# The last pair of examples joins the Toom-Cook scheme, the last pairs take turns in two sets of PSUM banks, and setup work is cut into portions

## The chip, the core and the metric

The kernel runs on one core of a Trainium2 chip. The metric is the device time of one execution in microseconds (us). In the profile PE is TensorE (matmuls), PEld its weight loads, DVE is VectorE, ACT is ScalarE, POOL is GpSimd and SP is SyncE, whose queue issues the DMAs. PSUM is the memory that matmuls write[...].

## What is computed

For 128 examples with 64 channels and 1024 positions, `out = x + L3(L2(L1(L0(x))))`. Each layer is a one-dimensional convolution with three taps over 64 channels; its weight is scaled per example and input channel by a style vector `s`, and normalised per output channel:

```python
s = style @ mw.T + mb
weight = SCALE * w * s[:, None, :, None]
demod = lax.rsqrt(jnp.sum(weight * weight, axis=(2, 3)) + EPS)
weight = weight * demod[:, :, None, None]
# layer types: 'same', 'upsample', 'same', 'downsample', with fixed blurs
x = x + L0_cond_ref(...)          # all four layers, one after another
```

There is nothing nonlinear between the layers. For inner positions the four layers are therefore one convolution with nine taps and a constant, different for every example; a few positions at either end are computed layer by layer.

## The kernel before, in words

**Units of work.** Two examples make a pair (64 channels each, 128 partitions); there are 64 pairs, p = 0 to 63. Two pairs make a group of four examples, and the main loop goes through 32 groups, q = 0 to 31. A round of the loop makes the nine-tap weights of group q+2 and convolves pairs 2q to 2q+3 in part.

**Weights of a group.** `scale3`, `stage1`, `stage2` and `stage3` build them in three steps of matmuls (PSUM tiles psS, psR, psW), each brought to SBUF with a scale by ACT, or by ACT and VectorE in the first groups. The scales come from small tables of style and normalisation values (tA, tB, tC, t0, t02, t3). `residual` adds the identity that carries `+ x`, and `combine` forms three combinations of the taps (tile H, five VectorE instructions, lines 406 to 410).

**Convolution of a pair.** The nine taps fall into 3 x 3 parts, and the kernel multiplies the three-part polynomials in Toom-Cook's manner with five products instead of nine, each product a convolution with three taps. `pre1` and `pre2` form the input combinations from X: tile G on VectorE (lines 436 and 439), two slots of tile T on GpSimd (lines 443 and 444), the others on VectorE (lines 449 and 459). `convA12` and `convA3` run products 1 to 3 into psA; ACT copies them with scales (m1, m3; lines 505 to 507); `seed` combines them on VectorE (u and v at lines 515 and 516, then Y at line 526 and y1 at line 527). `seed` writes Y into PSUM, and `convB` adds products 0 and 4 on top of it by matmul. `output` (line 548) scales and shifts Y and y1 on ACT, and `store` sends the result off. Y is one tile of two banks, used by all pairs in turn: the seed of a pair waits until ACT has read the pair before it.

**The last pair.** Only pairs 0 to 62 take this way (`NT3 = NP - 1`). Pair 63 is convolved directly with its nine taps into a tile psD (`direct_taps`, line 572): four taps ahead of the last Toom-Cook pair's `convB`, five after it. `half_input` makes a halved copy of its input on ACT.

**Side work.** Style scales, normalisation and constants of the first 16 examples are made in the prologue, of the next 16 partly there, of the remaining 96 (REST) in the loop: `EXTRA[(q, 0)]` and `EXTRA[(q, 1)]` stand in the middle and at the end of round q, and `SLOTS[q]` gives small matmuls (psE) between the two products of a `convB`. The ends of the examples are computed in the same places in rounds 5 to 17 (`setup_x`, `setup0` to `setup3`, `ends0` to `ends3`, `rest0` to `rest3`).

**Order.** The order on every engine is the order in which the program issues instructions; no scheduler changes it. Each engine works through its own queue and waits at an instruction whose inputs or buffers are not ready. psA, and psR and psS of the prologue, share a pool of two buffers (`ps_conv`); the weight stages of the loop, psE and psD share one (`ps_w`).

Of the kernel before, what the change touches and what calls it, by code (L numbers as in the profile page):

```python
# [62 lines left out]
def kernel(  # L64
# [91 lines left out]
    Yv = Y[:, :, : 2 * NB].rearrange("c s (i j) -> c s i j", i=2)  # L156

    def zeros_to_y(sets, n):


        for i in range(sets):
            rows = HALF[i % 2]
            for cols in HALF:
                nc.tensor.matmul(  # L164
                    Y[cols, i % 2, :n], Z[rows, :C], Z[rows, :n], start=True, stop=True
                )
# [20 lines left out]
    def mod_scale(bs, src):  # L187
        m = mbs[:, :, None].to_broadcast([P, NL, bs.stop - bs.start])
        nc_v.scalar_tensor_tensor(
            sc[:, :, bs], by_layer(src, bs), SCALE, m, op0=ALU.mult, op1=ALU.add  # L190
        )
        nc_v.tensor_mul(ssq[:, :, bs], sc[:, :, bs], sc[:, :, bs])
# [28 lines left out]
    def var_newton(bs):  # L221

        newton(var[:, :, bs], dm[:, :, bs], nw[:, :, bs])
# [25 lines left out]
    def tables_s(bs):  # L249

        table(nc_g, tB, bs, ALT, DOWN, sc[:, 2, bs], sc[:, 1, bs])
        table(nc_g, t0, bs, ALT, ODD, sc[:, 0, bs], 1.0)
        table(nc_g, t02, bs, ALT, ODD, sc[:, 0, bs], -2.0)

    def tables_d(bs):
        first, last = slice(0, 2), slice(2, 4)
        table(nc_g, tC, bs, first, last, dm[:, 1, bs], dm[:, 0, bs])
        table(nc_g, t3, bs, ALT, ODD, dm[:, 3, bs], var[:, 3, bs])

    def tables(bs):  # L260
        table_A(bs, dm[:, 2, bs])
        tables_s(bs)
        tables_d(bs)
# [156 lines left out]
    NT3 = NP - 1  # L420

# [7 lines left out]
    def pre1(p):  # L429

        if p >= NT3:
            return
# [10 lines left out]
        nc_g.tensor_add(t[:, 2, :NJ], plane(g, 2), plane(g, 1))  # L443
        nc_g.tensor_sub(t[:, 3, :NJ], plane(g, 2), plane(g, 1))  # L444

    def pre2a(p, eng=nc_v):
        if p < NT3:
            X, t = Xs[p % NX], Ts[p]
            eng.tensor_sub(t[:, 4, :NJ], plane(X, 3), plane(X, 1))
            load(p + NX, slice(1, 3))  # L450

    def pre2b(p):
        if p >= NT3:
            return
# [10 lines left out]
    def product(p, m, ps):  # L465
# [3 lines left out]
        for g in range(3):  # L469
            for s, rows in enumerate(HALF):  # L470
                for h, cols in enumerate(HALF):
                    if m in (0, 4):
                        w = W[rows, r0, K * g + m // 2, :]
                    else:
# [3 lines left out]
                        ps[cols, s, :],  # L478
# [10 lines left out]
    def convA12(p):  # L489
        if p >= NT3:  # L490
            return
        ps = ps_conv.tile([P, 2, 512], F32, tag="u", name=f"psA{p}")
        m = [ps[:, :, i * NB : (i + 1) * NB] for i in range(3)]
        product(p, 1, m[0])
        product(p, 2, m[1])
        part[p] = m

    def convA3(p):
        if p >= NT3:
            return  # L500
        m = part[p]
        product(p, 3, m[2])
        m1 = m_tile("m1", p)
        m3 = m_tile("m3", p, (2, 2, NB))
        nc_a.activation(m1, m[0], AF.Copy, scale=-1.0)  # L505
# [4 lines left out]
    def seed1(p):  # L510
        if p >= NT3:
# [9 lines left out]
    def seed2(p):  # L521
        if p >= NT3:
# [3 lines left out]
        nc_v.tensor_add(Yv, u[:, :, None, :].to_broadcast([P, 2, 2, NB]), m3)  # L526
# [8 lines left out]
    def convB(p, between=None):  # L535
        product(p, 0, Yv[:, :, 0, :])
        if between:
            between()
        product(p, 4, Yv[:, :, 1, :])
# [3 lines left out]
    def output(p, s):  # L543

        b = 2 * p + s
        o = os[p][:, s, :]
        for dst, src in ((o[:, : 2 * NB], Y[:, s, : 2 * NB]), (o[:, 2 * NB :], y1s[p][:, s])):
            nc_a.activation(  # L548
                dst, src, AF.Identity, bias=oc[:, b : b + 1], scale=dm[:, 3, b : b + 1]
            )  # L550
# [3 lines left out]

    direct = {}

    def half_input(p):

        t = tpool.tile([P, 5, PL], F32, tag="T", name=f"X{p}_half")
        direct["half"] = t.rearrange("c m j -> c (m j)")[:, :NXC]  # L560
        nc_a.activation(direct["half"], Xs[p % NX], AF.Copy, scale=-0.5)

    def direct_taps(p, taps):
        if 0 in taps:
            direct["ps"] = unit(ps_w, "psD")
        W, X = Wq[p // 2][0], Xs[p % NX]
        for t in taps:
            src = direct["half"] if t % K == 2 else X
            for s, rows in enumerate(HALF):
                for h, cols in enumerate(HALF):  # L570
                    for n, i in enumerate((0, 2, 1)):
                        nc.tensor.matmul(  # L572
                            direct["ps"][s][cols, n * NB : (n + 1) * NB],
                            W[rows, p % 2, t, :],
                            plane(src, (i + t) % 3, NB * h + (i + t) // 3, NB)[rows],
                            start=(t == 0 and n == 0),
                            stop=(t == NT - 1),
                            skip_group_check=True,
                        )

    def direct_output(p):
        o = opool.tile([P, 2, HO], F32, tag="o", name=f"o{p}")
        for s in range(2):
            b = 2 * p + s
            src, d3, add = direct["ps"][s][:, :HO], dm[:, 3, b : b + 1], oc[:, b : b + 1]
            if s == 0:
                nc_a.activation(o[:, s], src, AF.Identity, bias=add, scale=d3)
            else:
                nc_v.tensor_scalar(o[:, s], src, d3, add, op0=ALU.mult, op1=ALU.add)
            nc.sync.dma_start(out[p, :, s], o[:, s])  # L590
# [29 lines left out]
    def vectors(bs, eng=nc_v):  # L620

        n = bs.stop - bs.start
        eng.tensor_mul(a1[:, bs], sc[:, 2, bs], sc[:, 1, bs])
        eng.tensor_mul(Da[:, bs], sc[:, 3, bs], dm[:, 2, bs])
        eng.tensor_mul(c0f[:, bs], dm[:, 1, bs], bb[:, 0:1].to_broadcast([P, n]))
        eng.tensor_mul(b1s[:, bs], sc[:, 2, bs], bb[:, 1:2].to_broadcast([P, n]))
        eng.tensor_mul(c2f[:, bs], sc[:, 3, bs], bb[:, 2:3].to_broadcast([P, n]))
# [67 lines left out]
    def blurred(g, src, k1, k3):  # L695

        for b, f in enumerate((k1, k3, k3, k1)):
# [3 lines left out]
    def setup_x():  # L701
        nc_v.tensor_tensor(Xm, Xe, spread(sc[:, 0, :], 8), op=ALU.mult)
# [7 lines left out]
    def setup1():  # L710
        blurred(g1, woi[:, 1], 0.25, 0.75)

    def setup2():
        blurred(g3, wio[:, 3], 0.125, 0.375)
# [105 lines left out]
    BOTH = nc_a, nc_v  # L820
    zeros_to_y(2, 512)
# [8 lines left out]
    tables_s(PART[0])  # L830
    var_matmul(PART[0], pm[0][1])
    blur(0, 1)
    var_root(PART[0], pm[0][1])

    zeros_to_y(6, 256)
# [4 lines left out]
    scale3(1)  # L840
    blur(1, 3)
    var_inverse(PART[0])
    var_newton(PART[0])
    tables_d(PART[0])
    vectors(PART[0], nc_g)
# [4 lines left out]
    pre1(0)  # L850
    stage2(0, None, BOTH)
    pre2a(0, nc_g)
    mod_matmul(PART[1], pm[1][0])
    mod_scale(PART[1], pm[1][0])
    zeros_to_y(2, 512)
    const_first(0, PART[0])
    pre1(1)
    pre2a(1, nc_g)
# [3 lines left out]
    var_root(PART[1], pm[1][1])  # L862
# [3 lines left out]
    var_inverse(PART[1])  # L866
# [5 lines left out]
    const_rest(2, PART[0], const_of(2, PART[0]))  # L872
    stage2(1, ps_conv)
    pre2b(0)
    convA12(0)
    convA3(0)
    pre1(2)
    pre2a(2, nc_g)
# [3 lines left out]
    pre2b(1)  # L882
# [3 lines left out]
    var_newton(PART[1])  # L886
    tables(PART[1])
    vectors(PART[1], nc_g)
    residual(1)
    combine(1)  # L890
    pre2b(2)
    pre1(3)
    nc.sync.dma_start(Xe, x_ends)
    zeros()
# [5 lines left out]
    def scales_and_constant(matmul, l):  # L900
        def f(ps):
            matmul(REST, ps[0])
            const_matmul(l, PART[1], ps[1])

        return f

    def const1(l):
        const_rest(l, PART[1], raw[turn[0]][:, 1, :])

    SLOTS = {  # L910
        0: (scales_and_constant(mod_matmul, 0), NL * n, n1),
        1: (scales_and_constant(var_matmul, 1), NL * n, n1),
        2: (lambda ps: const_matmul(2, PART[1], ps[0]), n1),
# [3 lines left out]
        8: (ends0, HB * 6, HB * 6),  # L917
        10: (ends1(0), HB * 5, HB * 5),
        11: (ends1(1), HB * 4, HB * 4),
        14: (ends2, HB * 8, HB * 8),  # L920
        16: (ends3, HB * 3, HB * 3),
    }
    def after(side):
        return raw[turn[0]][:, side, :]


    EXTRA = {
        (0, 1): lambda: (mod_scale(REST, after(0)), const1(0)),
        (1, 1): lambda: (var_root(REST, after(0)), const1(1)),
        (2, 0): lambda: var_inverse(REST, slice(0, 1)),  # L930
        (2, 1): lambda: (const_rest(2, PART[1], after(0)), var_inverse(REST, slice(1, 2))),
        (3, 0): lambda: var_inverse(REST, slice(2, 3)),
        (3, 1): lambda: var_inverse(REST, slice(3, 4)),
        (4, 0): lambda: (var_newton(REST), tables(REST), vectors(REST, nc_g)),
        (5, 0): setup_x,
        (5, 1): lambda: (const_rest(0, REST, after(0)), setup0()),
        (6, 0): setup1,
        (6, 1): lambda: const_rest(1, REST, after(0)),
        (7, 0): setup2,
        (7, 1): lambda: (const_rest(2, REST, after(0)), setup3()),  # L940
        (8, 1): lambda: rest0(0),
        (9, 0): lambda: rest0(1),
        (10, 1): lambda: rest1(0),
        (11, 1): lambda: rest1(1),
        (12, 1): lambda: rest1_bias(0),
        (13, 0): lambda: rest1_bias(1),
        (14, 1): lambda: rest2(0),
# [121 lines left out]
```

## Time and profile before

| | |
|---|---|
| median of three runs | 520.89 us (520.56 to 521.82) |
| the profiled execution's own time | 520.98 us |
| its span, first to last instruction | 519.2 us |
| busy: PE, DVE, ACT, POOL | 501.2, 459.7, 364.8, 158.4 us |
| granted TensorE clock, mean | 0.997 |
| moved by DMA | 70.92 MB, mean 137 GB/s |

"Busy" counts every moment in which at least one instruction of the engine is under way. A PE that is busy is not always at its best rate[...]. Every fp32 matmul of the program stands in the trace as two records: 12 matmuls of a product are 24 records. The listed durations of neighbouring VectorE instructions overlap slightly, so what an instruction costs its queue is the distance of two starts.

### The profile page before, as it was taken

What the parts mean: (1) busy time and instruction counts of PE and PEld (TensorE: products, weight loads), DVE (VectorE), ACT (ScalarE), POOL (GpSimd) and SP (SyncE); (2) the same over time, 40 slices, a digit from 0 to 9 for tenths busy, and PEclk for the clock granted to TensorE, in tenths of its full rate; (3) what the DMA queues carried; (4) which work ended last, traced back from release to release, by engine and by line L of the source; (5) the groups of instructions that cost most, each with busy time, mean ns of one, the idle gap of its engine ahead of it and who ended that gap; (6) DMA issues with size and microseconds to landing.
All of it is one profiled execution on the core that took longest, in us unless ns stands there. A gap on an engine that the chain in (4) does not pass through costs nothing.

```text
span 519.2 us, 28593 instructions
## 1 busy us (share of the span) xinstructions
PE 501.2 (97%) x12724; PEld 478.0 (92%) x12724; DVE 459.7 (89%) x839; ACT 364.8 (70%) x908; POOL 158.4 (31%) x201
## 2 busy tenths in 40 slices
PE   8998999997899999999999999999999999999996
PEld 4897999997899799999979999999999999999996
DVE  5999989999999999889989989999998898888750
ACT  3365787776675777777767767787777777777742
POOL 3678122384323323212331313332222221222100
PEclk9998999999999999999999999999999999999999
DMA  8215443453534544434544445554444444453122
GB/s 250 85 46 168 147 152 115 137 166 109 139 117 133 164 129 139 147 114 138 164 113 138 135 118 177 167 164 135 144 144 161 142 148 134 159 166 110 68 101 82
DMA packets 37163, 70.92 MB, mean 137 GB/s; under 512 B 4144, under 2 KB 28464, under 8 KB 37040
## 3 DMA queue, kind: packets, MB, share of 16 engines
q1 hardware_dynamic: 36960, 68.85, 43.2%
q8 instruction: 100, 1.64, 1.4%
q10 hardware_dynamic: 80, 0.25, 0.1%
q14 instruction: 23, 0.19, 0.1%
HBM read 35.46 MB, written 33.62 MB: 133 GB/s over the span
## 4 chain that ended last, share of the span: by engine, by line
PE 78%; DVE 15%; ACT 3%; issue 2%; DMA 1%; DVEq 0%; ACTq 0%
PE psA L477 25%; PE Y L477 19%; PE psR L331 13%; PE psW L368 11%; PE psS L300 5%; DVE Y L526 3%; PE psD L572 2%; PE psE L725 2%; DVE y L527 2%; DVE G L436 1%; DVE T L459 1%; ACT o L548 1%; DVE G L439 1%; PE Y L164 1%; DVE H L409 1%
## 5 line engine op out<-in xcount | busy, mean ns | idle before, releaser
L477 PE MATMUL psA<-T,H 64*64 64x170 f32 x4536 | 190.1, 304 | 0.0
L477 PEld LDWEIGHTS psA<-T,H 64*64 64x64 f32 x4536 | 173.5, 133 | 0.5 <-issue 0.3
L443 POOL TENSOR_TENSOR T<-G 128x342 f32<-128x342 f32 x63 | 59.1, 938 | 318.1 <-DVE G L439 243.7
L477 PE MATMUL Y<-T,Wf 64*64 64x170 f32 x3024 | 129.4, 306 | 10.2 <-DVE Y L526 10.2
L477 PEld LDWEIGHTS Y<-T,Wf 64*64 64x64 f32 x3024 | 114.3, 133 | 15.1 <-DVE Y L526 13.8
L548 ACT ACTIVATE o<-Y,oc,dm 128x340 f32<-128x340 f32 x126 | 80.1, 636 | 43.8 <-PE Y L477 41.5
L526 DVE TENSOR_TENSOR Y<-u,m 128x680 f32<-128x680 f32 x63 | 69.7, 1106 | 30.5 <-ACT o L548 30.5
L278 ACT ACTIVATE Wf<-psW,t 128x256 f32<-128x256 f32 (+1 forms) x252 | 75.3, 381 | 24.7 <-PE psW L368 24.4
L368 PE MATMUL psW<-R,par_oi 64*64 64x256 f32 (+3 forms) x1536 | 91.7, 350 | 0.4 <-ACT Wf L278 0.4
L331 PE MATMUL psR<-S,E 64*64 64x192 f32 (+1 forms) x2304 | 89.4, 299 | 0.3 <-ACT S L278 0.3
L331 PEld LDWEIGHTS psR<-S,E 64*64 64x64 f32 x2304 | 81.7, 133 | 1.3 <-ACT S L278 0.7
L368 PEld LDWEIGHTS psW<-R,par_oi 64*64 64x64 f32 x1536 | 73.6, 133 | 7.8 <-ACT Wf L278 1.1
L444 POOL TENSOR_TENSOR T<-G 128x342 f32<-128x342 f32 x63 | 73.4, 1165 | 0.0
L548 ACT ACTIVATE o<-y,oc,dm 128x170 f32<-128x170 f32 x126 | 66.4, 527 | 0.0
L278 ACT ACTIVATE R<-psR,tC 128x448 f32<-128x448 f32 x63 | 36.5, 630 | 40.7 <-PE psR L331 40.7
L436 DVE SCALAR_TENSOR_TENSOR G<-X 128x688 f32<-128x688 f32 x63 | 56.1, 891 | 0.1
L459 DVE TENSOR_TENSOR T<-G 128x684 f32<-128x684 f32 x63 | 55.1, 875 | 0.0
L527 DVE SCALAR_TENSOR_TENSOR y<-m,v 128x340 f32<-128x340 f32 x63 | 49.1, 779 | 0.0
L300 PE MATMUL psS<-wd,par_oi 64*64 64x192 f32 x768 | 40.3, 324 | 0.0
L505 ACT ACTIVATE m<-psA 128x340 f32<-128x340 f32 x63 | 28.9, 459 | 7.0 <-PE psA L477 4.1
L300 PEld LDWEIGHTS psS<-wd,par_oi 64*64 64x64 f32 x768 | 32.3, 134 | 1.5 <-ACT wd L278 0.6
L439 DVE SCALAR_TENSOR_TENSOR G<-X 128x342 f32<-128x342 f32 x63 | 33.4, 531 | 0.0
(131 smaller groups left out, 476.1 us busy)
## 6 DMA issues: line engine op xcount, KB each, us to landing
out<-o SPq DMA_DIRECT2D x128, 255.0 KB, 3.4
X<-in_x SPq DMA_DIRECT2D x60, 344.0 KB, 3.3
X<-in_x SPq DMA_DIRECT2D x60, 172.0 KB, 3.2
X<-in_x SPq DMA_DIRECT2D x4, 516.0 KB, 6.9
Xe<-in_x_ends SPq DMA_DIRECT2D x1, 512.0 KB, 4.7
par_oi<-in_params_oi SPq DMA_DIRECT2D x2, 208.0 KB, 5.3
par_io<-in_params_io ACTq DMA_DIRECT2D x1, 240.0 KB, 4.3
par_io<-in_params_io SPq DMA_DIRECT2D x1, 240.0 KB, 4.9
```

Source lines behind the costliest of these rows:

```text
L278: nc_a.activation(dst, src, AF.Copy, scale=f)
L300: nc.tensor.matmul(ps[r][cols, k * C : (k + K) * C], woi[rows, 2, k, :], src[rows, :], start=(k == 0), stop=(k == K - 1), skip_group_check ...
L331: nc.tensor.matmul(ps[r][cols, lo * C : (lo + m) * C], E[rows, e + 2, :], src[rows, a, :], start=(n == 0), stop=(n == 8), skip_group_check ...
L368: nc.tensor.matmul(ps[r][cols, (lo - t_lo) * C : (hi - t_lo) * C], woi[rows, 0, k, :], rt[c][rows, lo - k : hi - k, :], start=(k == order[0]),
L436: nc_v.scalar_tensor_tensor(g[:, PL:], X[:, : 2 * PL], 0.5, X[:, PL:], op0=ALU.mult, op1=ALU.subtract)
L443: nc_g.tensor_add(t[:, 2, :NJ], plane(g, 2), plane(g, 1))
L444: nc_g.tensor_sub(t[:, 3, :NJ], plane(g, 2), plane(g, 1))
L459: nc_v.tensor_sub(t[:, 0:2, :NJ], both(a, PL), both(b, 1))
L477: nc.tensor.matmul(ps[cols, s, :], w, Ts[p][rows, SLOT[m], j : j + NB], start=(g == 0 and m not in (0, 4)), stop=(g == 2), skip_group_chec ...
L526: nc_v.tensor_add(Yv, u[:, :, None, :].to_broadcast([P, 2, 2, NB]), m3)
L527: nc_v.scalar_tensor_tensor(y1, m3[:, :, 0, :], 2.0, v, op0=ALU.mult, op1=ALU.add)
L548: nc_a.activation(dst, src, AF.Identity, bias=oc[:, b : b + 1], scale=dm[:, 3, b : b + 1])
```

## The change

1. Pair 63 takes the Toom-Cook way too. `half_input`, `direct_taps` and `direct_output` go away; `pre1`, `pre2`, `convA`, `seed`, `convB` and `output` of pair 63 come in.
2. The last pairs get a second set of banks. When the weights of the last group are done, `ps_w` has no more use: two of its banks become Y2, for pairs 60 and 62, while pairs 61 and 63 keep Y. Four zero matmuls prepare Y2. The last two rounds are reordered: `convA12` of pair 63 comes ahead of `convB` of pair 61, the seeds of 62 and 63 come earlier, VectorE does the second output of pairs 61 and 62, and pair 63 is output in parts by ACT and VectorE together.
3. The style matmul for all examples after the first 16 is done once in the prologue (`LATER`) and copied to SBUF by ACT, instead of once there for 16 examples and once in slot 0 for 96.
4. The side work of the loop is cut into smaller portions and spread further: what GpSimd did in round 4 in one piece (tables and vectors of REST) goes in portions into rounds 1 to 5, VectorE's normalisation of REST into rounds 2 to 5 by layers, and the work on the ends, in the slots 8, 10, 11, 14 and 16 before, into the slots 9, 12, 14, 19 and 24, with its setup and rest steps in rounds 6 to 25.
5. In the prologue, `pre1` and `pre2a` of pairs 0 and 1 run on VectorE alone, `pre2a` of pair 2 as well; several steps change places, and the first half of round 0 does the second part of pair 1's seed ahead of the column work of pairs 3 and 4.

The core of the diff:

```diff
+    def y_bank(p, s):
+        return Y2[p][s] if p in Y2 else Y[:, s]
...
-    NT3 = NP - 1
...
-    def pre1(p):
-
-        if p >= NT3:
+    def pre1(p, eng=nc_g):
+
+        if p >= NP:
             return
...
-        nc_g.tensor_add(t[:, 2, :NJ], plane(g, 2), plane(g, 1))
-        nc_g.tensor_sub(t[:, 3, :NJ], plane(g, 2), plane(g, 1))
+        eng.tensor_add(t[:, 2, :NJ], plane(g, 2), plane(g, 1))
+        eng.tensor_sub(t[:, 3, :NJ], plane(g, 2), plane(g, 1))
...
+        if p in Y2:
+            for s in range(2):
+                nc_v.tensor_add(
+                    blocks(y_bank(p, s)[:, None, :]), uu[:, s : s + 1], m3[:, s : s + 1]
+                )
+        else:
+            nc_v.tensor_add(blocks(Y), uu, m3)
...
+    mod_matmul(LATER, pm[1][0])
 
-    zeros_to_y(6, 256)
+    zeros_to_y(4, 256)
...
+    nc_a.copy(raw[0][:, 0, :n_later], pm[1][0][:, :n_later])
...
+    mod_scale(PART[1], raw[0][:, 0], LATER)
+    for of in (table_B, vector_a1, table_0, table_02, vector_b1, vector_c2):
+        of(PART[1])
     stage2(0, None, BOTH)
-    pre2a(0, nc_g)
-    mod_matmul(PART[1], pm[1][0])
-    mod_scale(PART[1], pm[1][0])
+    pre1(0, nc_v)
+    pre2a(0)
...
     EXTRA = {
...
-        (4, 0): lambda: (var_newton(REST), tables(REST), vectors(REST, nc_g)),
-        (5, 0): setup_x,
-        (5, 1): lambda: (const_rest(0, REST, after(0)), setup0()),
-        (6, 0): setup1,
...
+        (1, 0): lambda: (table_B(REST), vector_a1(REST)),
+        (1, 1): lambda: (var_root(REST, after(0)), const_rest(0, PART[1], after(1))),
+        (2, 0): lambda: (var_inverse(*layers(2, 3)), table_0(REST), vector_b1(REST)),
+        (2, 1): lambda: (const_rest(1, PART[1], after(0)), var_newton(*layers(2, 3))),
+        (3, 0): lambda: (table_A(REST, dm[:, 2, REST]), table_02(REST), vector_c2(REST)),
+        (3, 1): lambda: (const_rest(2, PART[1], after(0)), var_inverse(*layers(1, 2))),
+        (4, 0): lambda: (var_inverse(*layers(0, 1)), vector_Da(REST)),
+        (4, 1): lambda: (var_newton(*layers(0, 2)), table_C(REST), vector_c0(REST)),
+        (5, 0): lambda: var_inverse(*layers(3, 4)),
+        (5, 1): lambda: (
+            const_rest(0, REST, after(0)),
+            var_newton(*layers(3, 4)),
+            table_3(REST),
+        ),
...
         if q == NQ - 1:
+            seed(p + 1)
+        output(p, 1, nc_a if q < NQ - 1 else nc_v)
+        if q == NQ - 1:
+            store(p, 0)
+            store(p, 1)
+
+            convB(p + 1)
+            for i in (2, 0, 1):
+                for r, eng in enumerate(BOTH):
+                    output(p + 1, r, eng, ((i, i + 1),))
             for i in range(2):
-                store(p, i)
-            direct_taps(p + 1, range(4, NT))
-            direct_output(p + 1)
+                store(p + 1, i)
             break
...
+            store(p, 0)
+            seed2(p + 1)
+            pre2(p + 3)
+            store(p, 1)
+            pre2b(p + 2)
+            pre1(p + 4)
...
+        if q == NQ - 2:
+            convA12(p + 3)
         side = SLOTS.get(q)
         convB(p + 1, (lambda: slot(*side)) if side else None)
+        if q == NQ - 2:
+            seed(p + 2)
...
+        if c == NQ - 1:
+
+            banks = unit(ps_w, "Y2")
+            Y2[p + 2] = Y2[p + 4] = banks
+            zeros_to_y(2, 2 * NB, p + 2)
```

## The prediction

> **What bounds the kernel now.** The page first: engines, the chain that ended last, TensorE's costliest groups.
>
> ```profile
> PE 501.2 (97%) x12724; PEld 478.0 (92%) x12724; DVE 459.7 (89%) x839; ACT 364.8 (70%) x908; POOL 158.4 (31%) x201
> PE 78%; DVE 15%; ACT 3%; issue 2%; DMA 1%; DVEq 0%; ACTq 0%
> L477 PE MATMUL Y<-T,Wf 64*64 64x170 f32 x3024 | 129.4, 306 | 10.2 <-DVE Y L526 10.2
> ```
>
> TensorE bounds most of the span, but it waits for one thing, VectorE's seed of Y. The windows view by rounds (starts of stage2 from the timeline) says where:
>
> ```profile
> 97.41:112.61 15.20, 14.63 (x393) 13.77 (x385) 14.91 (x26) 11.22 (x29) 8.01 (x11) 1.00 0.40 107
> 112.61:130.06 17.45, 14.70 (x396) 13.87 (x391) 17.31 (x29) 11.36 (x30) 9.54 (x14) 1.00 0.48 142
> 130.06:146.29 16.23, 14.79 (x396) 14.43 (x391) 15.93 (x34) 11.46 (x30) 4.52 (x5) 1.00 0.48 133
> 146.29:162.18 15.89, 14.79 (x397) 14.43 (x391) 15.62 (x30) 11.47 (x30) 4.83 (x5) 1.00 0.45 129
> 392.71:407.10 14.39, 14.39 (x393) 14.13 (x386) 12.66 (x25) 11.21 (x29) 3.60 (x4) 1.00 0.48 148
> ```
>
> (Length, then PE, PEld, DVE, ACT, POOL busy.) A late round takes 14.39 us, all TensorE; rounds 4 to 7 take 15.2 to 17.5 with VectorE full: there VectorE bounds. Its timeline gives the first seeds of rounds 5 to 8:
>
> ```profile
> 123.55 1.04 DVE L526 TENSOR_TENSOR Y<-u,m 128x680 f32<-128x680 f32 x1
> ...
> 139.78 1.04 DVE L526 TENSOR_TENSOR Y<-u,m 128x680 f32<-128x680 f32 x1
> ...
> 155.64 1.07 DVE L526 TENSOR_TENSOR Y<-u,m 128x680 f32<-128x680 f32 x1
> ...
> 172.16 1.06 DVE L526 TENSOR_TENSOR Y<-u,m 128x680 f32<-128x680 f32 x1
> ```
>
> Distances 16.23, 15.86 and 16.52; by starts, the side work between them is 2.26, 1.90 and 2.52. The rest is 13.97, 13.96 and 14.00: **a saturated VectorE round costs 13.97 us**, only 0.42 under TensorE's 14.39. Side work beyond 0.42 a round, plus TensorE's own side matmuls, lengthens the round.
>
> The end has a third limit:
>
> ```profile
> 499.99 5.59 PE psD L572 x92
> 507.75 6.93 PE psD L572 x116
> DVE o L589 <- PE psD L572: 11.8, 1, 11.8
> ```
>
> In the chain of waits the direct convolution's 216 records take about 12.6 us, 58 ns each; a Toom-Cook product takes 0.87 us for 24, 36 ns.[...]
>
> [...] y1 takes 0.50 us alone and 1.22 beside GpSimd's T, two instructions of H 1.15 instead of 0.56. So moving column work off GpSimd returns part of its price.
>
> **The tail.** Removed: 216 direct records (12.6 us) and the half copy (1.05 on ACT, hidden). Added for pair 63: five products, 120 records at 36 ns (4.3 us), and on VectorE line 436 0.79, 439 0.42, 449 0.42, 459 0.78, u and v 0.84, Y 0.86, y1 0.42, by starts. Followed queue by queue from `convB(59)`, which ends at 489.75:
> - Four zero matmuls into Y2: eight 64x512 records took 1.09 at 16 us, so 340 columns take 0.7. They need psW empty, which it is at 488.7. `convA(61)` ends at 493.0.
> - VectorE does `pre2(62)`, then the added `pre1(63)`, to 490.4; u, v and Y2 for pair 60, with GpSimd's T beside them, to 492.5, early enough; then `combine(31)` as before, to 496.4. `convB(60)` ends at 494.8, `convA(62)` at 497.4.
> - `convA12(63)` needs the psA buffer of pair 61, and VectorE reaches u and v of 61 only after `combine(31)` and `pre2(63)`, at 498.5: a new wait of 1.1, with `convB(61)` and `convA3(63)` queued behind it. The matmuls end at 500.3, `convB(61)` at 502.0, `convA3(63)` at 502.9; Y2 for 62 was ready at 501.5, so `convB(62)` ends at 504.6.
> - ACT's m3 of 63 comes behind `output(61, 0)`, at 504.0; Y of 63 at 504.9; `convB(63)` ends at 506.7. The last part of the output, 170 columns (0.53 on ACT), ends at 507.35.
>
> Before, the last output ended at 515.52. The stores behind it are the same size and keep their 3.7 us. **Tail: -8.1 us** (-9 to -5.5[...]).
>
> **The loop, rounds 2 to 25.** TensorE's side matmuls are the same work in other slots, and cost what they did; removed is slot 0's style matmul (1.3), but VectorE bounds that round, so I count it as nothing. What GpSimd gets in portions, about 1 to 2.6 us a round, lies in its idle time (7 us ahead of a T). Round 4 before also had 8 us of GpSimd tables, which pushed T onto H: its distance was 17.41 - 13.97 - 2.33 = 1.1 above the rule. VectorE's stall before, distances minus 14.39 and minus the slot of that round: 0.55, 0.82, 3.02, 1.69, 1.32, 1.98 (rounds 2 to 7) and 0.98 (13), 10.4 in all. After, side work per round, from rows of the same kind (reciprocal 0.67 of 96 columns, Newton 0.75 for one layer and 1.0 for two, constants 0.29 or 0.46, tA 0.45, half of `setup_x` 0.6, half of `setup1` 0.72, `setup0` 0.67, `setup3` 0.62, each `rest0` 1.1, `rest1` 0.96, each bias step 1.29, each `rest2` 1.37):
>
> | round | side | after 0.42 and the slot | stall |
> |---|---|---|---|
> | 1 | 0.56 | -0.71 | 0 |
> | 2 | 1.71 | 1.19 | 0.48 |
> | 3 | 1.41 | 0.89 | 0.89 |
> | 4 | 1.67 | 1.25 | 1.25 |
> | 5 | 1.88 | 1.31 | 1.31 |
> | 6, 7 | 1.06 each | 0.49 each | 0.98 |
> | 8 | 0.67 | 0.25 | 0.25 |
> | 9, 10 | 1.72, 1.82 | -0.64 (slot 1.94), 1.40 | 0.76 |
> | 11 | 0.72 | 0.30 | 0.30 |
> | 12 to 16 | 0.96, 0, 0.96, 1.29, 1.29 | slots 1.6, 1.4; lead up to 1.6 | 0.14 |
> | 17 | 1.44 | 1.02 | 1.02 |
> | 19 to 25 | two of 1.37, 0.7, 1.2 | slots 2.6, 2.7 cover | 0 |
>
> Sum 7.4. **Loop: -3.0 us**; up to -5.5 if shorter side work lets VectorE regain its lead[...].
>
> **Prologue and round 0.** VectorE gains seven T instructions of 342 columns (0.42 each by starts, 2.9 us)[...]. The style matmul for 112 columns in place of 16 has no row; by 16 records of 96 columns in 1.34 us it costs at most 1.4 more, less two sets of zeros dropped (0.9), and delays `stage1(0)` by 0 to 0.5. The ACT copy of 448 columns (as R, 0.63) falls ahead of S at 11.84 and costs nothing there. On VectorE, H(1) can start at 33.6, behind the last ACT part of its weights (33.2) and the residual; H takes 3.0[...], then line 449, u, v 1.26, line 459 0.78, G 1.22, normalisation of the second part 1.6: pair 1's seed at 42.7, before at 44.47. The gap of 2.6 us ahead of `convB(1)` shrinks to about 1.3. But `pre2(3)`, `pre2b(2)` and `pre1(4)`, 3.2 us, are only put behind that seed. From it to seed 3 the queue holds, by starts, columns 1.98 + 1.22 + 1.2 + 1.22, u, v, Y, y1 of pair 2 2.54, residual and H 3.4, scales 1.06, columns 2.42, u and v 0.84, with y1 of pair 1 0.42: 16.3[...]. Seed 3 starts at 60.0 to 61.5, before at 60.70: TensorE waits for it in rounds 0 and 1 instead of once, and `convB(3)` starts where it did. SP's loads of X for pairs 4 to 7 are issued some microseconds apart from before, long ahead of use; the load of Xe and GpSimd's memsets go into round 1, used from round 6 on. **Start: 0** (-1.5 to +2).
>
> **Sum.** -8.1 - 3.0 + 0 = -11.1 on a span of 519.2; the profiled execution took 520.98 (1.78 around the span), the median is 520.89. So **509.8 us**.
>
> **Rivals.**
> - *The debt only moves.* VectorE does the same side work, and in saturated rounds each microsecond reaches TensorE wherever it stands; for it speaks 0.42 of room a round, against it that rounds 17 to 31 have idle VectorE. Tail -8.1, start +1.5: 514.3.
> - *The banks turn, but the seeds are late*, i.e. the change doesn't do what it says at the end: VectorE's queue (pair 63's column work, the split Y, two outputs) holds seeds 61 to 63, each `convB` waits about 1 us more. Tail -5, loop -3: 513.
> - *VectorE becomes the bound in rounds 2 to 25 (slower).* [...] With +0.44 the table's stalls become about 13.3, still a gain. The point is a round of about 14.65, +0.7; at +1.0 some 20 rounds add 0.56 each, the stalls reach 24.5 and the sum is +6: 527. Only round 4 before, with 8 us of GpSimd work, was that slow.
>
> **How the numbers follow.** Forecast 0.63, first rival 0.2, second 0.12, third 0.05. Differences within 0.3% (1.6 us) can hardly be told from none here; little lies there. Faster 0.93, same 0.02, slower 0.05. The forecast's own ends (-9 - 5.5 - 1.5 to about -4) and the first two rivals give 505 to 515.5.
>
> **What would show it.** Right: no psD, last output some 3.7 us ahead of the end, 120 records in its place, a wait ahead of pair 63's psA; first seeds of rounds 2 to 5 some 15.3 to 15.7 us apart and of 6 to 8 about 14.9; DVE full until round 11 or so. Wrong: rounds above 15.7 through 10 (third rival), or `convB` of 61 to 63 waiting over 1 us each (second); a start that ends `convB(3)` beyond 64 or before 60.

## The result, and the profile after

The changed kernel takes 518.68 us in the median of six runs (515.94 to 519.51), the kernel before 521.41 (520.56 to 521.82): ratio 0.9943, interval 0.9918 to 0.9969. It is faster, but by about 2.9 us (518.19 against 521.07 when both were run again) where 11.1 were forecast. Its runs spread over 3.6 us, those of before over 1.3. The profiled execution is the fastest of the six: 515.94 us, span 514.1, mean granted clock 0.993.

The page of after, in the lines that answer to those of before (engines, chain that ended last, TensorE's matmuls into Y):

```profile
PE 492.9 (96%) x12612; PEld 467.9 (91%) x12612; DVE 476.7 (93%) x869; ACT 364.0 (71%) x908; POOL 159.7 (31%) x196
PE 65%; DVE 20%; ACT 3%; issue 2%; DVEq 0%
L481 PE MATMUL Y<-T,Wf 64*64 64x170 f32 x3072 | 131.3, 307 | 12.0 <-DVE Y L547 10.9
```

The 216 direct records are gone and the 120 of pair 63 are in, but VectorE's share of the chain rose from 15 to 20%, and TensorE waits for its seeds of Y as long as before (10.9 us against 10.2). The windows by rounds, 4 to 7 and a late one:

```profile
99.18:114.52 15.34, 14.86 (x392) 14.27 (x387) 15.17 (x28) 11.25 (x29) 5.32 (x6) 1.00 0.48 140
114.52:130.53 16.01, 14.70 (x397) 13.88 (x391) 15.80 (x28) 11.37 (x30) 7.08 (x8) 1.00 0.48 133
130.53:146.51 15.98, 14.78 (x396) 14.42 (x390) 15.74 (x30) 11.46 (x30) 6.15 (x7) 1.00 0.44 136
146.51:161.50 14.99, 14.79 (x397) 14.43 (x392) 14.82 (x27) 11.47 (x30) 4.84 (x5) 1.00 0.47 143
389.44:403.86 14.42, 14.42 (x392) 13.90 (x386) 13.88 (x24) 11.23 (x29) 4.50 (x5) 1.00 0.54 155
```

(Length, then PE, PEld, DVE, ACT, POOL busy, the granted clock, and DMA.) VectorE is still full through round 7. The first seeds of rounds 5 to 8 in VectorE's timeline:

```profile
124.04 1.02 DVE L547 TENSOR_TENSOR Y<-u,m 128x680 f32<-128x680 f32 x1
...
139.99 1.05 DVE L547 TENSOR_TENSOR Y<-u,m 128x680 f32<-128x680 f32 x1
...
154.99 1.03 DVE L547 TENSOR_TENSOR Y<-u,m 128x680 f32<-128x680 f32 x1
...
169.99 1.06 DVE L547 TENSOR_TENSOR Y<-u,m 128x680 f32<-128x680 f32 x1
```

They are 15.95, 15.00 and 15.00 us apart; less the forecast's side work (1.88, 1.06, 1.06) that is 14.07, 13.94 and 13.94. The rule of 13.97 us for a saturated VectorE round holds, as far as the side work was forecast rightly.

Cut by the starts of stage2 of groups 0, 10 and 31 (the last two open rounds 8 and 29), the profiles show where the gain is and where it went. The last column is VectorE's idle time within the stretch from stage2(0) to stage2(10), its length less its busy time there.

| kernel | stage2(0) at | to stage2(10) | to stage2(31) | to the end | VectorE idle |
|---|---|---|---|---|---|
| before | 12.42 | 149.76 | 316.89 | 40.1 | 5.72 |
| after | 11.79 | 149.71 | 317.26 | 35.3 | 6.40 |
| after, again | 13.49 | 150.61 | 317.34 | 35.4 | 7.80 |

The whole gain is in the end, 4.8 us. The loop's shorter rounds gained nothing: rounds 2 to 7 took 91.37 us in place of 93.89, but from stage2(0) to the start of round 2 after took 58.34 in place of 55.87.

### The profile page after: what moved, and what is told of

Same layout as the page of the kernel before. It is cut to its first block, busy times and chain, and to the rows that moved or that the text cites. A ratio compares the mean times of both kernels' runs of the same rounds, so it can differ in the third digit from the quotient of the medians.

```text
span 514.1 us, 28399 instructions
## 1 busy us (share of the span) xinstructions
PE 492.9 (96%) x12612; PEld 467.9 (91%) x12612; DVE 476.7 (93%) x869; ACT 364.0 (71%) x908; POOL 159.7 (31%) x196
## 4 chain that ended last, share of the span: by engine, by line
PE 65%; DVE 20%; ACT 3%; issue 2%; DVEq 0%
PE psA L481 21%; PE Y L481 18%; PE psR L337 11%; PE psW L374 9%; PE psS L306 4%; DVE Y L547 3%; DVE T L463 3%; DVE y L548 2%; DVE G L440 2%; PE psE L724 2%; ACT o L572 2%; DVE G L443 1%; DVE u L528 1%; DVE T L453 1%; DVE H L413 1%
## 5 line engine op out<-in xcount | busy, mean ns | idle before, releaser
L481 PE MATMUL psA<-T,H 64*64 64x170 f32 x4608 | 193.9, 304 | 1.0 <-DVE v L529 1.0
L481 PEld LDWEIGHTS psA<-T,H 64*64 64x64 f32 x4608 | 176.9, 133 | 2.2 <-issue 1.6
L447 POOL TENSOR_TENSOR T<-G 128x342 f32<-128x342 f32 x62 | 57.0, 920 | 312.8 <-DVE G L443 266.7
L481 PE MATMUL Y<-T,Wf 64*64 64x170 f32 x3072 | 131.3, 307 | 12.0 <-DVE Y L547 10.9
L481 PEld LDWEIGHTS Y<-T,Wf 64*64 64x64 f32 x3072 | 115.9, 133 | 18.0 <-DVE Y L547 15.0
L572 ACT ACTIVATE o<-Y,oc,dm 128x340 f32<-128x340 f32 (+1 forms) x126 | 79.8, 633 | 48.0 <-PE Y L481 47.2
L547 DVE TENSOR_TENSOR Y<-u,m 128x680 f32<-128x680 f32 x62 | 67.2, 1083 | 17.2 <-ACT o L572 17.0
L448 POOL TENSOR_TENSOR T<-G 128x342 f32<-128x342 f32 x62 | 82.0, 1323 | 0.0
L548 DVE SCALAR_TENSOR_TENSOR y<-m,v 128x340 f32<-128x340 f32 x64 | 60.2, 940 | 0.0
L463 DVE TENSOR_TENSOR T<-G 128x684 f32<-128x684 f32 x64 | 56.3, 881 | 0.0
L528 DVE SCALAR_TENSOR_TENSOR u<-psA,m 128x340 f32<-128x340 f32 x64 | 32.1, 502 | 0.8 <-ACT m L520 0.8
```

The costliest lines, as they stand in the source:

```text
L447: eng.tensor_add(t[:, 2, :NJ], plane(g, 2), plane(g, 1))
L448: eng.tensor_sub(t[:, 3, :NJ], plane(g, 2), plane(g, 1))
L463: nc_v.tensor_sub(t[:, 0:2, :NJ], both(a, PL), both(b, 1))
L481: nc.tensor.matmul(ps[s][cols], w, Ts[p][rows, SLOT[m], j : j + NB], start=(g == 0 and m not in (0, 4)), stop=(g == 2), skip_group_check=True,
L547: nc_v.tensor_add(blocks(Y), uu, m3)
L548: nc_v.scalar_tensor_tensor(y1, m3[:, :, 0, :], 2.0, v, op0=ALU.mult, op1=ALU.add)
```

## The experiments

Medians are compared with those of before taken beside them (520.88 to 521.17). In the expectations "stage2(2)" means the start of round 2, and "the last full round" and "round 31" start at stage2(31).

**The end alone.** The kernel before, with only points 1 and 2 of the change. 

> The kernel before with only the end changed (pair 63 by Toom-Cook, the banks of Y by turns, the last rounds reordered); prologue and side work of the loop as before. My theory says that the end is worth what the trace of after shows from the start of the last full round on, 35.3 us in place of 40.1: a median 4.5 to 5.2 us below before, about 516.3, with outputs 61 and 63 each held by ScalarE and VectorE waiting for each other. Rival: the end by itself is worth the forecast 8.1 us, and the rest of the change spoils it: 512.8. Second rival: the end needs the rest of the change to be early enough, and gives under 3 us.

 Measured: 515.92 us, ratio 0.9899 (0.9886 to 0.9912), 515.61 to 516.10. This alone beats the whole change. The end is worth 5.1 us, not 8.1; the rest of the change costs 2.3 us in the median and brings the spread.

**After, again.** 

> The changed kernel once more, for its spread. Theory of the clock (the several short gaps of TensorE in the prologue let the clock drop in some executions and not in others, by their phase): times spread over 3 to 4 us, 515.5 to 519.5, and the span goes with the granted clock between 60 and 70 us. Rival: the spread of the first six was an accident: all within 1.5 us.

 Measured: 518.19 (515.99 to 519.07), ratio 0.9936 (0.9917 to 0.9954). The execution profiled here took 518.60 us. Windows of after, from 60 to 70 us, then of after again:

```profile
60.00:65.00 5.00, 2.59 (x46) 2.54 (x49) 5.00 (x9) 0.95 (x3) 4.21 (x5) 0.80 0.69 206
65.00:70.00 5.00, 5.00 (x124) 5.00 (x124) 3.73 (x8) 3.68 (x10) 2.72 (x4) 0.86 0.48 135
```

```profile
60.00:65.00 5.00, 2.20 (x49) 1.74 (x42) 5.00 (x8) 2.18 (x7) 2.88 (x3) 0.81 0.71 202
65.00:70.00 5.00, 5.00 (x76) 4.92 (x72) 3.61 (x6) 1.50 (x4) 3.15 (x6) 0.51 0.27 82
```

The clock falls to 0.80 and 0.86 in one, to 0.81 and 0.51 in the other, and VectorE (its busy time is the fourth figure of a line) goes from full to 3.7 and 3.6 of 5 us. The timeline of after again shows the cause on TensorE and the effect on VectorE:

```profile
63.81 1.98 PE L481 MATMUL Y<-T,Wf 64*64 64x170 f32 x24 [2.80 <-DVE Y L547]
```

```profile
70.66 0.94 DVE L547 TENSOR_TENSOR Y<-u,m 128x680 f32<-128x680 f32 x1 [2.05 <-ACT o L572]
80.44 0.88 DVE L547 TENSOR_TENSOR Y<-u,m 128x680 f32<-128x680 f32 x1 [1.37 <-ACT o L572]
```

Behind a wait of 2.80 us, half of `convB(3)` takes 1.98 us in place of 1.10. The pair is output late, and VectorE, which bounds this stretch, waits 2.05 and 1.37 us for ACT to free Y. In the first profile of after these waits were 1.27 and 0.83; stage2(0) to stage2(10) differs by 0.9 us, and from there to the end the two executions agree within 0.1. Over the twelve executions of after, time and mean clock go together only in part (515.94 us at 0.993, 517.89 at 0.996, 519.51 at 0.990): the mean also counts falls at the very end, and not the slow first 10 us that the last section shows.

**TensorE kept busy in the gaps.** Ahead of `convB(1)` and `convB(3)`, zero matmuls into an idle bank:

```diff
+        if q < 2:
+            fill(f"fill{q}", 2 + 2 * q, 512)
```

> After, with zero matmuls into an idle bank ahead of convB(1) (8 records of 512 columns' worth, about 2 us) and ahead of convB(3) (twice that), so that TensorE stays busy where it waited for VectorE in rounds 0 and 1; they compute nothing that is used. Theory of the clock: the granted clock stays at 1.0 from 60 to 70 us, stage2(2) starts at 68.0 in place of 70.1, and the median is 1.5 to 2.5 us below after, with a narrower spread. Rival: VectorE's queue sets the start whatever TensorE does; stage2(2) at 70, median within 0.7 us of after. Second rival: the fill is late itself and delays the convB behind it, +1 us.

 Measured: 516.94 (516.40 to 517.01), ratio 0.9917 (0.9904 to 0.9930). The spread shrinks from 3.1 to 0.6 us, and the clock stays up:

```profile
60.00:65.00 5.00, 4.48 (x77) 2.62 (x73) 5.00 (x9) 2.38 (x8) 2.34 (x2) 1.00 0.62 156
65.00:70.00 5.00, 5.00 (x144) 5.00 (x137) 5.00 (x8) 3.38 (x9) 4.33 (x7) 1.00 0.57 185
```

Stage2(0) to stage2(10) takes 148.83 us, and VectorE is idle 4.37 us of it. Round 2 starts at 70.44 us, not at the expected 68.0, because stage2(0) was late (14.07); from there it takes 56.37 us, after 58.34 and 59.33. The gain of 1.25 us is just short of the range: round 3 gave part back (15.51 in place of 14.52).

**The seed first.** In round 1, `seed(3)` goes ahead of `pre2(5)` and `pre1(6)`:

```diff
+        if q == 1:
+            store(p, 0)
+            seed(p + 1)
+            pre2(p + 3)
```

> After, with one block of VectorE's queue in round 1 reordered: u, v and Y of pair 3 go ahead of the column work of pairs 5 and 6 (2.4 us of T and G instructions) that stood in front of them. Theory of the clock: the third gap, 2.8 us ahead of convB(3), shrinks to under 0.7, the clock stays at 1.0 from 60 to 70 us, convB(3) starts at about 60.0 in place of 62.4 and stage2(2) at 66 to 67.5 in place of 70.1 to 72.8; median 3 to 4.5 us below after, about 514.5, spread under 2.5 us. Rival: VectorE bounds everything up to round 10, so what is won here comes back as longer gaps in rounds 2 to 7; stage2(10) starts where it did (161.5) and the time is within 1 us of after.

 Measured: 516.72 (515.68 to 517.08), ratio 0.9912 (0.9899 to 0.9924). The gap shrank to 0.22 us, the clock stayed at 1.00 and round 2 began at 67.61, but the gain on after is 1.5 us where 3 to 4.5 were expected: rounds 2 to 7 then took 94.88 us in place of 91.37. Both theories had part: the clock theory the cause (148.70 us to stage2(10), VectorE idle 4.32), the rival the size, for VectorE's queue takes back what is only put off.

**The old start.** After, with the prologue and round 0 of before (points 3 and 5 undone, the style matmul for 96 columns back in slot 0). 

> After, with the prologue and round 0 of the kernel before (column work on GpSimd, style matmul for the last columns in slot 0); loop and end as after. Theory: the start is what spoils the change. stage2(2) at 68.3 to 68.6, the loop's 2.1 us and the end's 4.8 us add up: median 513.5 to 514.3, spread under 1.5 us. Rival: the loop's gain only made up for the late start, and with the old start the rounds 2 to 10 cost what they did before: 515.9, as with the end alone.

 Measured: 514.21 (513.90 to 514.44), ratio 0.9870 (0.9855 to 0.9884). The theory holds: the new start costs 4.0 us in the median. The profile has stage2(0) at 12.10, then 147.41, 317.28 and 35.3 us. The window from stage2(0) to stage2(10):

```profile
12.10:159.51 147.41, 140.09 (x3612) 132.91 (x3616) 144.04 (x260) 101.70 (x260) 71.81 (x98) 1.00 0.44 130
```

VectorE is busy for the same 144.04 us as before, but idle for 3.37 instead of 5.72. Against the end alone (515.92) the median is 1.7 us lower.

**Column work back on GpSimd.**

```diff
-    pre1(0, nc_v)
-    pre2a(0)
+    pre1(0)
+    pre2a(0, nc_g)
...
-    pre2a(2)
+    pre2a(2, nc_g)
```

(and pair 1 likewise.) 

> After, with the T instructions of pairs 0 and 1 and the third one of pair 2 back on GpSimd, in the same places of the program: the last part of the change undone by itself. Theory: they lie ahead of pair 1's seed, so convB(1) starts 1 to 2.5 us later (44.5 to 46)[...], but from there to convB(3) little changes (18.5 in place of 19.1), and the slump after the last gap stays: stage2(2) at 70.5 to 73, median 0 to 2 us above after. Rival: it is these instructions on VectorE that make seed 3 late; without them convB(3) waits under 1 us and the median is 2 us or more below after.

 Measured: 518.06 (515.65 to 519.31), ratio 0.9935 (0.9913 to 0.9957): no change. `convB(1)` came 31.2 us after stage2(0), in after 31.5. My expectation of a later seed failed, and so did the rival: which engine does these T instructions is worth nothing here. VectorE's busy time fell to 141.76, and its idle time rose to 7.67.

**Both together.** 

> After, with the T instructions of pairs 0 to 2 back on GpSimd and the seed of pair 3 ahead of the column work of pairs 5 and 6. Theory (from stage2(0) to stage2(10) the time is VectorE's busy time plus its waits): with these T instructions on GpSimd VectorE was busy 141.9 us and waited 7.7, with the seed first it was busy 144.5 and waited 4.3; both together should give 141.9 + 4.3 = 146.2 to 147.2 us, where after took 149.7 to 150.6 and the old start 147.4. Median 514.3 to 515.5. Rival: [...] 148.5 or more, and the median is that of seed3_first, 516.7.

 Measured: 516.31 (515.26 to 516.85), ratio 0.9912 (0.9899 to 0.9925), and 148.73 us to stage2(10): the rival. Busy and idle times of two kernels can't be combined; here they were 143.21 and 5.52, and 3.6 us of the idle time lay between stage2(0) and round 0, as with these T instructions alone (3.7; with the seed first alone 2.5).

**The style matmul later.**

```diff
-    mod_matmul(LATER, pm[1][0])
...
     stage2(0, None, BOTH)
     pre1(0, nc_v)
     pre2a(0)
+    mod_matmul(LATER, pm[1][0])
```

> After, with the style matmul of the last 112 columns, its copy and what reads it moved behind stage2(0). In the profiles so far it ran in front of stage1(0) and took 1.4 to 1.8 us, and stage2(0) began at 11.8 to 14.1 us, late whenever TensorE's first 10 us ran at half rate. Theory: stage1(0) then starts at 9.5 to 10.0, stage2(0) at 11.4 to 12.2 with little spread, and from there to stage2(10) it takes 149.5 to 150.8 as after; median 0.7 to 1.5 us below after, 517. Rival: the style matmul was what kept TensorE busy, without it the rate rises later; stage2(0) at 12.5 to 14, median within 0.5 us of after.

 Measured: 518.68 (516.92 to 520.02), ratio 0.9955 (0.9940 to 0.9970). Stage2(0) did start at 12.08, but the stretch behind it took 150.49, with new waits of VectorE of 1.43, 0.98 and 0.67 us between 15 and 23 us: moved, not saved. This profile also shows a gap of 2.79 us ahead of `convB(3)` after which the clock stayed at 1.00 and half of `convB(3)` took 1.10.

**G of pair 0 earlier.** With the seed first, and `pre1(0)` ahead of stage2(0) as in before:

```diff
+    pre1(0)
     stage2(0, None, BOTH)
-    pre1(0, nc_v)
-    pre2a(0)
+    pre2a(0, nc_g)
```

> The kernel with the seed of pair 3 first, and besides the G instructions of pair 0 ahead of stage2(0) (its T instructions on GpSimd), as in the kernel before. With the seed first, VectorE still waited 1.03 us for stage2(0) with nothing queued that it could do, where the old start had G there. Theory (VectorE's queue from stage2(0) to stage2(10) sets the time, its waits included): this wait goes, and the stretch takes 147.4 to 148.0 us in place of 148.7; median 0.6 to 1.2 us below seed3_first. Rival: the new start has something else that the old one has not, and the stretch stays at 148.4 or more.

 Measured: 515.82 (515.35 to 516.58), ratio 0.9896 (0.9877 to 0.9915), and 148.26 us to stage2(10), between the two. The wait at stage2(0) went and 1.05 us came at the next stage. What remains against the old start, 0.9 us, I could not assign.

**Halves of the last outputs apart.** A tile `o` for each half (not shown in the diff), and Y2 for pairs 61 and 63:

```diff
-            Y2[p + 2] = Y2[p + 4] = banks
+            Y2[p + 3] = Y2[p + 5] = banks
```

> After, with an output tile for each half and Y2 given to pairs 61 and 63 in place of 60 and 62, so that the two halves of the last outputs share no tile: ScalarE and VectorE no longer have a reason to wait for each other. Theory: output(61, 1) no longer waits 1.3 us, u and v of 63 and Y(63) come 0.8 us earlier, convB(63) ends at 507.2 in place of 508.0, and the last output 0.7 us behind it at about 507.9 in place of 510.05: the time 1.5 to 2.2 us below after. Rival: the halves are bound by something else (the banks, ScalarE's own queue), and the time stays within 0.5 us of after.

 Measured: 515.39 (515.19 to 516.64), ratio 0.9897 (0.9883 to 0.9912). Since the start scatters, the end is what counts: 34.25 us from stage2(31), in after 35.3. The chain in order of time at the end of after:

```profile
506.04 2.00 PE Y L481 x48
508.04 0.02 issue
508.06 0.50 ACT o L572
508.56 0.03 issue
508.59 0.46 DVE o L574
509.05 0.02 issue
509.08 0.50 ACT o L572
509.58 0.03 issue
509.60 0.45 DVE o L574
```

and with the halves apart:

```profile
506.14 2.30 PE Y L481 x48
508.44 0.03 issue
508.47 0.46 DVE o L574
```

In after the four last parts run one behind the other, ACT and VectorE by turns, 2.0 us from the matmuls to the end of the output. Apart they run side by side, 0.85 us. `convB(63)` came no earlier, against the expectation: u(63) now waited 0.82 us for ACT's copy m3.

**Only `o` apart.** 

> After with separate output tiles for the halves, and Y2 left with pairs 60 and 62, so that the halves of the last output still lie in one tile Y that ScalarE and VectorE both only read. Theory: two readers of one PSUM tile are kept in program order as the two writers of o are, so VectorE's waits behind ScalarE in outputs 61 and 63 stay, and the stretch from stage2(2) to the end is 443.6 to 444.1 as after. Rival: only the shared o tile orders them; 442.7 to 443.1 as with both separated.

 Measured: 517.94 (515.33 to 518.55), ratio 0.9924 (0.9897 to 0.9951); from round 2 to the end 443.8 us as in after, and VectorE's waits stay:

```profile
511.08 0.45 DVE L574 TENSOR_SCALAR o<-Y,dm,oc 128x170 f32<-128x170 f32 x1 [1.18 <-ACT o L572]
512.10 0.45 DVE L574 TENSOR_SCALAR o<-Y,dm,oc 128x170 f32<-128x170 f32 x1 [0.56 <-ACT o L572]
```

So the one tile Y, which both engines only read, is enough to hold them in program order. Whether the shared `o` alone would be enough too was not tried.

**u and v of pair 63 earlier.** In `convA3(63)`, ahead of the product:

```diff
+        if p == NP - 1:
+            uv[p] = seed1_of(p, m1s[p], m[1])
         product(p, 3, [m[2][:, s] for s in range(2)])
```

> The kernel with separate output tiles and Y2 for pairs 61 and 63, and besides u and v of pair 63 put ahead of its third product and the copies of it on ScalarE. In the run before, VectorE waited 0.8 us with u(63) for ScalarE's copy m3, which it does not need; both read one PSUM tile. Theory: readers of one tile on two engines are kept in program order, so now u(63) runs at about 502.2, Y(63) starts 0.8 us earlier against the start of round 31, and the end (from the start of stage2(2)) takes 442.0 to 442.3 in place of 442.9. Rival: the third product then waits for u and v (it writes the same tile), and nothing is gained: 442.7 to 443.2.

 Measured: 518.43 (517.80 to 519.49), ratio 0.9952 (0.9940 to 0.9965); from round 2 to the end 444.4 us, 1.5 worse than with the halves apart alone. It is the rival, and more than it said: in VectorE's queue this place lies behind the half output of pair 61, and the third product waited for it.

```profile
506.71 1.10 PE L481 MATMUL psA<-T,H 64*64 64x170 f32 x24 [1.98 <-DVE v L537]
```

**The best of both ends.** The old start with the halves apart. 

> The kernel with the start of before and the loop and end of after, with separate output tiles for the halves and Y2 given to pairs 61 and 63. Theory: the two gains add, since they lie at opposite ends: 1.1 us below the one with the old start (514.2), so 512.8 to 513.4, the best so far. Rival: the earlier end of VectorE's work is lost to the stores, 514.0 or more.

 Measured: 513.43 (512.96 to 513.77), ratio 0.9856 (0.9844 to 0.9869), with the next one the fastest kernel here: 7.5 us below before, about 5 below after. It lies at the upper edge of what was expected, and the two gains add.

**The same with u and v in the right place**, behind `seed(62)` in VectorE's queue. 

> The same, and u and v of pair 63 put into VectorE's queue right behind the seed of pair 62, ahead of the half output of pair 61 (in early_u they stood behind it, and the third product waited 2 us for them). Theory: u(63) no longer waits for ScalarE's m3; the third product waits 0.3 to 0.5 us for v, Y(63) starts 0.5 to 0.8 us earlier, and the time is 0.3 to 0.7 us below old_start_split. Rival: the third product and with it convB(62) and m3 move by as much as Y(63) gains: within 0.2 us of it or slower.

 Measured: 513.50 (513.03 to 514.19), ratio 0.9859 (0.9847 to 0.9872): the rival. The third product waited 0.45 us, and what the last seed gained was not seen in the time.

## Why the prediction was wrong, by its steps

**The bound was right, but its stretch was cut too late.** VectorE does bound the early rounds, and a saturated round is 13.97 us. The table's stalls of after are near: rounds 2 to 7 measure 5.0 us above 14.39 each, about 0.65 of it for the slots' matmuls, where 4.9 without the slots were forecast. With the old start, the start that the forecast assumed, they measure 6.2, so part of the close fit of after is luck.

But the saturated stretch begins in the prologue, not in round 2. From stage2(0) to stage2(10) the end alone takes 149.71 us and the old start 147.41, 2.3 less (1.7 in the medians); the new start spends 2.3 to 3.2 us of it (149.71 to 150.61). Less work for VectorE is not what saves the 2.3: it is busy for 143.96 us with the end alone and 144.04 with the old start. Three waits for Y in rounds 0 to 2 are gone, which before and the end alone have and the old start has not. In before, between 32.9 and 84 us (total, times, longest):

```profile
DVE Y L526 <- ACT o L548: 2.2, 3, 1.0
```

The first of them comes behind `convB(1)`, half of which took 1.98 us there: the clock stood at 0.67 from 45 to 50 us in the profile of before and at 1.00 in that of the old start. So part of the 2.3 may be the clock; hardly all, for the seven executions of before with a mean clock of 1.000 took 520.39 us on average, only 0.6 less than the profiled one.

**Start, forecast 0 (-1.5 to +2), measured about +4.** The steps up to pair 3's seed were near: in after, pair 1's seed began at 42.38 us (42.7 forecast), seed 3 at 61.33 (60.0 to 61.5), `convB(3)` at 62.41 (62.16 in before); only the gap ahead of `convB(1)`, which was to shrink to about 1.3, measured 2.12. The 16.3 us of queue between these seeds measured 18.95; the forecast's allowance of 1 to 2.5 us on top, for VectorE instructions that take longer beside GpSimd's T, was an estimate, and three such instructions (T 1.58 us, G 1.58, y1 1.22, else 0.86, 0.86 and 0.51) took 2.1 us of it. The failed step is the last, "`convB(3)` starts where it did", taken as harmless: in the profiles of after round 2 begins at 70.13 and 72.82 us, in before at 68.29. One gap of 2.58 us had become three (2.12, 1.43 and 2.79), and the price of a gap is not only its length. The forecast's own sign, a `convB(3)` that ends beyond 64, could not tell: in before it ends at 64.93, in after at 66.80.

TensorE's granted clock fell behind gaps of about 2.8 us ahead of `convB(3)` in six of seven profiles (0.51 to 0.86 in windows of 5 us) and behind gaps of 2.0 to 2.6 us ahead of `convB(1)` in seven of fifteen (0.66 or 0.67). The length does not tell which: behind 2.12 us ahead of `convB(1)` the clock from 45 to 50 us was 1.00 in after and 0.66 in after again. The clock records of before and after show more. The clock first rises at 10.73 and 8.42 us, and every later change lies a whole number of steps of 3.413 us behind that: half clock began after 10 steps in before and after 16 in after, lasted one, and full clock then lasted 138 and 130. By these steps, half clock followed each one in which TensorE was idle for 2.07 us or more (2.07 in before, 2.79 and 2.17 in after, the kernels' last steps aside), and none in which it was idle for 1.48 us or less; no step lies between. Two pairs of steps in before, around its gap of 2.58 us and around one of 2.75 us in round 5:

```profile
41.45:44.87 3.42, 1.35 (x36) 1.03 (x28) 3.42 (x5) 2.25 (x7) 3.42 (x15) 1.00 0.92 282
44.87:48.28 3.41, 2.90 (x36) 2.29 (x38) 3.41 (x4) 0.00 (x0) 2.78 (x4) 0.50 0.63 206
119.96:123.37 3.41, 1.93 (x52) 1.51 (x44) 3.41 (x7) 2.74 (x9) 0.43 (x1) 1.00 0.44 119
123.37:126.79 3.42, 2.14 (x60) 2.14 (x64) 3.42 (x5) 0.24 (x1) 1.98 (x2) 1.00 0.67 194
```

The first gap leaves 2.07 us of one step idle (its length less PE's 1.35), and the next step runs at half clock. The second is longer, but the end of a step cuts it into 1.48 and 1.28 us, and the clock stays at 1.00.

The clock cost 0.9 to 1.8 us of the stretch (after's two profiles against the one with the gaps filled). A second term is a later stage2(0): it started at 12.42 us on average in the five profiles with the old prologue, at 13.23 in the ten with the style matmul in front of `stage1(0)`, from 11.79 to 14.11. That the style matmul, forecast at 0 to 0.5, causes this is not shown. Stage2(0) is late where TensorE's first matmuls run slowly for longer: the 24 records of `stage1(0)` took 1.21 us in after, where stage2(0) began at 11.79, and 2.15 with the gaps filled, where it began at 14.07. Where the slow rate ended at about the same time, both prologues are equally early: 12.68 us with the style matmul (both together; `stage1(0)` from 10.79 in 1.20 us), 12.42 and 12.72 without (before and the end alone; from 10.38 in 1.35 and from 10.70 in 1.33). VectorE's wait of 1.0 us at stage2(0) is a third, worth 0.4. The 0.9 us left are open. The range for the start came from what VectorE's queue holds; the clock stood in no term, though the profile of before shows 0.67 behind its own gap.

**The end, forecast -8.1 (-9 to -5.5), measured -4.8 to -5.1.** All steps to `convB(62)` held: the wait for psA was 0.99 (1.1), and the products and `convB` ran at the forecast 36 ns a record (why a direct record took 58 was not shown). Measured from stage2(31), these terms were short:

| step | short by |
|---|---|
| u and v of 63 run behind ACT's m3, not before it | 0.85 |
| m3 itself | 0.45 |
| `convB(63)` | 0.3 |
| last output: four parts by turns, not one part of 170 columns | 1.4 |
| stores behind it, 4.05 instead of 3.7 | 0.35 |

Together 3.35. The fourth is shown by the run with the halves apart (1.1 us at the end). For the first, two runs moved u and v ahead: it shifts the wait to the third product, so the term was a real cost and not a slip of order. The forecast read data dependences alone; the program also orders two engines that only read one PSUM tile (waits of 1.18 and 0.56 us with only `o` apart).

**Loop, forecast -3.0, measured -2.15 in the trace from round 2 to stage2(31).** With the old start it is only -1.0 (409.78 us in place of 410.78), so part of what the late start of after loses comes back there. Both lie inside the range. The mis-sized term is what before lost: 9.4 us in rounds 2 to 7 by distances of seeds without the slots, but 7.55 by lengths of rounds with them. In rounds 2 and 3 the distances gave stalls of 0.55 and 0.82, and the rounds took 14.52 and 14.60 us; where a seed still has a lead, its distance is no stall of TensorE. Rounds 8 to 28 cost 0.4 more than before, forecast 1.5 more.

**The rivals.** "The debt only moves" (514.3) had the sign of the start and the mechanism that seed3_first showed, but not the clock. "Seeds late" (513) did not happen: no `convB` of 61 or 62 waited, that of 63 waited 1.1. "VectorE becomes the bound" (527), a saturated round of about 14.65 from many small portions on GpSimd, did not happen: that round stayed at 13.94 to 14.07; rounds 5 and 6 of after took 16.0 us, past its sign of 15.7, but before lost more there (17.45 and 16.23).

## What to carry to other kernels

Mark where an engine is saturated from its first full microsecond, and sum its busy and idle time over all of that stretch: a gain inside it counts only if nothing ahead of it adds an idle wait. Price a TensorE gap by what follows it as well as by its length; gaps that left at most 1.48 us idle in a step of 3.41 us were followed by no fall of the clock in before and after. When two engines share the last output, give each its own tiles for what it reads as well as for what it writes.

## What the runs showed of the hardware that was not expected

- The same gap can be followed by half clock in one profile and not in another: behind 2.12 us ahead of `convB(1)` the granted clock was 0.66 from 45 to 50 us in after again and 1.00 in after, and behind 2.79 to 2.80 us half of `convB(3)` took 1.10 us in one profile, 1.43 and 1.98 in others. In before and after the clock changed only at steps of 3.41 us counted from its first rise, at 10.73 and 8.42 us, and half clock followed the steps with 2.07 us of idle time or more, none with 1.48 or less. It lasted one step of 3.41 us there, the kernel's end left out; in after again the windows from 60 to 70 us (0.81 and 0.51) give about 6.8 us. In six profiles a gap of 1.4 us ahead of `convB(2)` was followed by a clock of 1.00.
- In the first 10 us the granted clock is listed as 1.00 while matmuls run at about half their later rate, for the traces of before and after hold no record of the clock before its first rise (10.73 and 8.42 us): the same 16 zero records took 1.09 us in after and 1.99 in after again:

```profile
8.78 1.09 PE L168 MATMUL Y<-Z 64*64 64x256 f32 x16
```

```profile
9.69 1.99 PE L168 MATMUL Y<-Z 64*64 64x256 f32 x16
```

This is most of why stage2(0) began at 11.79 in one and 13.49 in the other: from the style matmul on, it took 4.41 and 5.49 us.
